# Ordering the FFN weights' preparation on VectorE behind the first inner k blocks

## The chip, the cores and the metric

The kernel runs on one core of a Trainium2 chip. The metric is the device time of one execution in microseconds (us). A core has five engines that run their own instruction queues side by side: TensorE (PE; PEld is its weight load), VectorE (DVE), ScalarE (ACT), GpSimd (POOL) and SyncE (SP, here a queue that only issues transfers). Semaphores order instructions of different engines; instructions of one engine follow each other.

## The reference

A graph layer of 384 nodes with 1024 features, followed by a gated FFN whose weights and activations are quantised to 8 bits. Cut to what matters here:

```
q = x @ wq.T + bq;  k = ...;  v = ...            # x after a layer norm
q2 = (q @ wiq.T + biq) in 16 heads of 64;  k2 = (k @ wik.T + bik);  v2 = (v @ wiv.T + biv)
scores = q2 @ k2.T / 8 + mask                     # mask: -inf where there is no edge
x = x + (softmax(scores) @ v2) @ wo.T + bo

def weight_fake_quant(w):                         # one scale per row
    scale = max(abs(w), axis=1) / 127
    return clip(round(w / scale), -128, 127) * scale

h = act_fake_quant(silu(xq @ wfq(w_gate).T) * (xq @ wfq(w_up).T))    # xq: quantised layer norm of x
out = x + h @ wfq(w_down).T                       # w_gate, w_up: 352 x 1024; w_down: 1024 x 352
```

## The kernel before

The first phase makes q, k, v and q2. Two output blocks of 128 features at a time are computed by a scheme with seven products instead of eight (`project2`): sums of weight halves (`left_sums`, L169 to L173) and of activation quarters (`right_sums`, L157) go in, and VectorE and ScalarE combine the seven results (L200 to L224). Each product is four matmuls of a 128x192 result, shown as eight records[...]. The function takes turns with other VectorE work: the sums for the next pair and the building of the edge mask (L412 to L422), which GpSimd scatters to memory (L425) and reads back (L439).

The second phase is attention in eight head pairs p (L667 on). For p the kernel computes scores (L603), adds the mask and takes the row minimum on VectorE (L609), takes the exponential on ScalarE (L613), normalises on VectorE (L621, L623), turns the result on TensorE (L633), copies it on ScalarE (L635) and multiplies with v2 (L641). Between these steps TensorE is filled with other matmuls: in even p a quarter of v2 (`inner_v`, L580, evacuated by VectorE at L586), in odd p the next two k2 blocks (`inner_k`, which calls `project2`). The first two k2 blocks, `inner_k(0)`, are made ahead of the loop: L664 and L665. The weights of the next `inner_k` are loaded at L79, those of `inner_v` at L570.

The preparation of the FFN weights is a generator, `ffn_weights`. There are fourteen row units: three of w_gate, three of w_up, eight of w_down. For each one, `load_row` (L517) issues the load of a row block into one of three buffers named `row`, two units ahead; `quantise_rows` takes the row maximum on VectorE (L496, tile `wmx`), scales it (L497), takes the reciprocal (L499, tile `wrs`), multiplies on ScalarE with an 8-bit result (L502, tile `w8b`, one buffer) and turns it to bf16 on VectorE (L504, tile `wqi`). When the generator is next advanced, TensorE transposes it (L533 or L540) and ScalarE copies the result out (L534, L541, L542). A `row` buffer is free for the next load when its L502 has run.

`prepare` (L701) advances that generator at fixed points of the loop over p: three times in p = 0, once in p = 1 and 3, twice in the others.

What sets the order: TensorE, SP and GpSimd keep the order in which the program text issues instructions in the whole kernel (a manual schedule for these three). VectorE and ScalarE are ordered by the text in the first phase only up to the loop's set-up; from the end of that context a planner orders their instructions at build time by its own costs. It may move an instruction of the preparation ahead of instructions that the text has earlier, when its operands allow it. In the built program the first L496 stands in the last but one pair of q2's projection, far ahead of the place where `prepare` is called, and four L496 more lie ahead of the last sum of `inner_k(0)`. The loads of the third and later row blocks stand in SP's queue where the text has them; the loads of the second `inner_k`'s weights stand behind the fourth and fifth row loads, which wait for the first and second L502.

Of the kernel before, what the change touches and what calls it, by code (L numbers as in the profile page):

```python
# [28 lines left out]
ALU = mybir.AluOpType  # L29
# [27 lines left out]
def row_bcast(ap, n):  # L57
    return bass.AP(tensor=ap.tensor, offset=ap.offset, ap=[[0, P], [1, n]])
# [3 lines left out]
def gnn_ffn_kernel(ctx: ExitStack, tc: tile.TileContext, a: dict, out: bass.AP):  # L62
    nc = tc.nc
# [13 lines left out]
    def load_w(name, j):  # L77
        wt = w.tile([P, F], F32, name="wt")
        nc.sync.dma_start(wt, a[name][j])  # L79
        return wt  # L80
# [97 lines left out]
    def project2(wa, wb, sums, right, da, db, bias_a, bias_b, pool, name, aside=None):  # L178


        half = HK * P
        s1, s2 = sums
        b11, b21, b22, t1, t2, t3, t4 = right
        a1, a2, b1, b2 = da[:, :HN], da[:, HN:], db[:, :HN], db[:, HN:]

        def product(left, r):
            z = pool.tile([P, HN], F32, name=name)
            for k in range(HK):
                nc.tensor.matmul(  # L189
                    z, left[:, k * P : (k + 1) * P], r[:, k, :], start=(k == 0), stop=(k == HK - 1)  # L190
                )
                yield
            return z

        def other():
            if aside:
                aside()

        def add(dst, z, b, with_):
            nc.vector.scalar_tensor_tensor(dst, z, b, with_, op0=ALU.add, op1=ALU.add)  # L200

        z = yield from product(wa[:, :half], b11)
        nc.scalar.copy(a1, z)  # L203
        other()
        z = yield from product(s2, t2)
        nc.vector.tensor_add(b1, z, a1)
        other()
        z = yield from product(wa[:, half:], b21)
        add(a1, z, bias_a, a1)
        nc.vector.tensor_sub(wa[:, half:], wa[:, half:], s2)  # L210
        other()
        z = yield from product(s1, t1)
        nc.scalar.activation(b2, z, AF.Identity, bias=bias_b)  # L213
        add(a2, z, bias_a, b1)
        other()
        z = yield from product(wb[:, :half], t3)
        nc.vector.tensor_add(b1, z, b1)
        nc.vector.tensor_add(b2, b2, b1)
        other()
        z = yield from product(wa[:, half:], b22)  # L220
        nc.vector.tensor_add(a2, z, a2)
        other()
        z = yield from product(wb[:, half:], t4)
        add(b1, z, bias_b, b1)  # L224
        other()
        yield

    def in_turn(*steps):
        steps = list(steps)
        while steps:  # L230
            for s in list(steps):
                try:
                    yield next(s)
                except StopIteration:
                    steps.remove(s)

    def run(steps):
        for _ in steps:
            pass
# [6 lines left out]
    with ph1_stack:  # L246
# [208 lines left out]
        for i, (name, o) in enumerate(todo[:-1]):  # L455
            (wa, wb), sums = wq_next, sums_next
            right, dst, cols = work[name]
# [49 lines left out]
    def ffn_weights():  # L507

        units = [(name, m, ic) for m, name in enumerate(("L0_ffn_w_gate", "L0_ffn_w_up")) for ic in range(3)]
        units += [("L0_ffn_w_down", 2, c) for c in range(KC)]  # L510
        ahead = []

        def load_row():
            name, m, j = units[len(ahead)]
            i0, rows = ICS[j] if m < 2 else (j * P, P)
            wn = rows_p.tile([P, F], F32, name="row")
            nc.sync.dma_start(wn[:rows, : F if m < 2 else I], a[name][i0 : i0 + rows, :])  # L517
            ahead.append(wn)

        load_row()  # L520
        load_row()
        for u, (name, m, j) in enumerate(units):
            wn = ahead[u]
            if len(ahead) < len(units):
                load_row()
            if m < 2:
                i0, rows = ICS[j]
                wT = (wgT, wuT)[m]
                wq = quantise_rows(wn, rows, F, w_scale[:rows, m, j : j + 1])
                yield  # L530
                pt = ps_tp.tile([P, KC, P], BF16, name="tp")
                for k in range(KC):
                    nc.tensor.transpose(pt[:, k, :rows], wq[:rows, k * P : (k + 1) * P], ident_b[:rows, :rows])  # L533
                nc.scalar.copy(wT[:, :, i0 : i0 + rows], pt[:, :, :rows])  # L534
            else:
                wq = quantise_rows(wn, P, I, wd_scale[:, j : j + 1])
                yield
                pt = ps_tp.tile([P, 3, P], BF16, name="tp")
                for ic, (i0, rows) in enumerate(ICS):
                    nc.tensor.transpose(pt[:rows, ic, :], wq[:, i0 : i0 + rows], ident_b)  # L540
                nc.scalar.copy(wdT[:, 0:2, j * P : (j + 1) * P], pt[:, 0:2, :])  # L541
                nc.scalar.copy(wdT[:96, 2, j * P : (j + 1) * P], pt[:96, 2, :])  # L542

    with ExitStack() as ph:
# [4 lines left out]
        def inner_k(p):  # L549

            k2 = pair_p.tile([P, 2, N], F32, name="k2")
            if p == 0:
                (wa, wb), sums = wq_next, sums_next
            else:
                wa, wb = (load_w("wik", p + j) for j in range(2))
                sums, steps = left_sums(wa, wb, turned)
                run(steps)
            b0 = 4 * KC + p
            return k2, project2(
                wa, wb, sums, k_right, k2[:, 0], k2[:, 1], bias[:, b0 : b0 + 1], bias[:, b0 + 1 : b0 + 2],  # L560
                ps_mm, "mm",
            )
# [85 lines left out]
        def out_group(wo, t, g, ks, pm):  # L648
            gs = slice(g * 512, (g + 1) * 512)
            for k in ks:  # L650
                nc.tensor.matmul(  # L651
                    pm, outT[:, k, t * P : (t + 1) * P], wo[k][:, gs], start=(k == 0), stop=(k == KC - 1)
                )
                yield

        def take(steps, n):
            for _ in range(n):
                if next(steps, "end") == "end":
                    return

        NP = H // 2
        prep = ffn_weights()

        k2_next, first = inner_k(0)  # L664
        run(first)  # L665
        e_before = None
        for p in range(NP):  # L667
            if p % 2 == 0:
                k2 = k2_next
            sc = scores(q2[:, p], k2[:, p % 2])  # L670
            wg = weigh(p - 1, e_before) if p else iter(())
            if p == NP - 1:
                early = [(t, g, ps_mm.tile([P, 512], F32, name="mm")) for t, g in ((0, 0), (0, 1))]
                fill, n = (s for t, g, pm in early for s in out_group(wo, t, g, range(NP - 2), pm)), 2 * (NP - 2)
            elif p % 2:
                k2_next, fill = inner_k(p + 1)
                n = 7 * HK + 1
            else:
                fill, n = inner_v(p // 2), NT * KC
            if p == NP - 2:  # L680

                x = act.tile([P, NT, F], F32, name="actT")
                bo_b = w.tile([P, F], F32, name="wt")
                nc.sync.dma_start(bo_b, row_bcast(a["L0_gnn_bo"], F))
                for t in range(NT):
                    nc.sync.dma_start(x[:, t, :], a["x"][t * P : (t + 1) * P, :])
                for t in range(NT):
                    for g in range(2):
                        gs = slice(g * 512, (g + 1) * 512)
                        nc.vector.tensor_add(x[:, t, gs], x[:, t, gs], bo_b[:, gs])  # L690
                wo = [load_w("wo", k) for k in range(KC)]
            done = 0

            def fill_to(sixteenths):
                nonlocal done
                upto = n * sixteenths // 16
                take(fill, upto - done)
                done = upto


            def prepare(at):  # L701
                if at in ((2, 6, 12) if p == 0 else (2,) if p in (1, 3) else (2, 14)):
                    take(prep, 1)


            fill_to(3 if p % 2 else 2)
            prepare(2)
            next(sc)
            for m in (6, 9, 12):
                fill_to(m)  # L710
                prepare(m)
                take(wg, 1)
            fill_to(14)
            prepare(14)
            run(fill)

            e_before = next(sc)
            take(wg, 1)
# [285 lines left out]
```

## Time and profile before

| what | value |
|---|---|
| time, median of 3 runs | 375.97 us (375.29 to 376.20) |
| the profiled execution | 376.68 us, its span 374.9 us |
| mean granted TensorE clock | 0.994 |
| PE busy | 358.8 us, 96% of the span |
| VectorE busy | 260.2 us, 69% |
| ScalarE busy | 112.8 us, 30% |
| TensorE waited for VectorE's L171 | 1.8 us, once |
| VectorE's L496 | 14 times, 11.4 us busy, 9.5 us idle before |

Busy time is the time in which an engine runs an instruction; the span goes from the first instruction to the last. The chain of waits is followed back from the last instruction and tells which engine sets the end at each time. A busy share of 96% on TensorE means that time can be lost or won only where TensorE stands still, some 16 us in all, 10 of them in the last 31 us.

### The profile page before, as it was taken

The page shows a single profiled execution, that of the slowest core. Times are in us where ns is not written, and L with a number is a line of the kernel's source. Part 1 is how long each engine was busy: PE and PEld are TensorE (multiplying, and loading weights), DVE is VectorE, ACT ScalarE, POOL GpSimd, SP SyncE. Part 2 cuts the span into 40 slices and gives each one's busy share as a digit, 9 for nine tenths or more (in the row PEclk, how much of TensorE's full clock was granted, in tenths as well). Part 3 has the DMA queues.
Part 4 walks back from the last instruction along what each step waited for, and adds up shares of the span by engine and source line. Part 5 has one row for each costly group of instructions (what it writes and reads, how often), then busy time and mean ns, then how long its engine had stood idle before and what let it go on. Part 6 is the DMA issues. An engine that isn't in the chain of part 4 may idle for free.

```text
span 374.9 us, 5872 instructions
## 1 busy us (share of the span) xinstructions
PE 358.8 (96%) x2113; PEld 298.9 (80%) x2113; DVE 260.2 (69%) x788; ACT 112.8 (30%) x264; POOL 72.1 (19%) x81
## 2 busy tenths in 40 slices
PE   8999999999999999799999999999999999999981
PEld 7899999999999999698877878686866545449660
DVE  5868888878889985998487457717492521199785
ACT  2152000100000000123672546446444523034330
POOL 6110254455444544210000000000000000000003
PEclk9999999999999999999999999999999999999997
DMA  8995433343333357148070040040294000000004
GB/s 236 393 376 213 150 114 112 116 133 114 112 112 115 112 170 247 57 119 289 21 231 32 19 129 23 18 171 1 101 375 132 31 0 2 0 0 3 1 0 168
DMA packets 17805, 44.50 MB, mean 119 GB/s; under 512 B 3263, under 2 KB 8401, under 8 KB 17393
## 3 DMA queue, kind: packets, MB, share of 16 engines
q1 hardware_dynamic: 15104, 39.46, 31.1%
q0 software_dynamic: 2672, 4.68, 4.2%
q8 instruction: 16, 0.26, 0.3%
q14 instruction: 13, 0.10, 0.1%
HBM read 41.91 MB, written 2.21 MB: 118 GB/s over the span
## 4 chain that ended last, share of the span: by engine, by line
PE 76%; DVE 12%; DMA 6%; ACT 3%; issue 1%; SPq 0%; DVEq 0%; ACTq 0%
PE p L189 34%; PE mm L580 7%; PE mm L189 6%; PE sc L641 4%; PE tp L633 4%; PE mm L651 3%; PE sc L651 3%; PE mm L814 3%; PE sc L603 3%; PE mm L303 3%; DMA row<-in_L_ffn_w_gate_dram 2%; DMA row<-in_L_ffn_w_down_dram 2%; DMA wt<-in_wik_dram 2%; PE sc L814 1%; DVE s L609 1%; DVE wmx L496 1%
## 5 line engine op out<-in xcount | busy, mean ns | idle before, releaser
L425 POOL DMA_INDIRECT mask_d<-value,place x51 | 56.9, 1115 | 66.3 <-DVE place L422 50.8
L189 PE MATMUL p<-actT,wt 128*128 128x192 f32 x360 | 65.9, 326 | 0.5 <-DVE actT L200 0.5
L189 PEld LDWEIGHTS p<-actT,wt 128*128 128x128 f32 x360 | 59.6, 190 | 0.8 <-DVE actT L200 0.8
L580 PE MATMUL mm<-wt,actT 128*128 128x256 f32 x192 | 46.1, 384 | 0.0
L580 PEld LDWEIGHTS mm<-wt,actT 128*128 128x128 f32 x192 | 34.8, 190 | 7.8 <-issue 2.2
L613 ACT ACTIVATE e<-s,mn 128x384 f32<-128x384 f32 x48 | 29.0, 605 | 26.4 <-DVE mn L609 26.4
L609 DVE CUSTOM_DVE_ANT_0 s<-sc,mask 128x384 f32<-128x384 f32 x48 | 24.5, 551 | 13.0 <-PE sc L603 12.8
L189 PE MATMUL p<-x_right,s 128*128 128x192 f32 x176 | 32.2, 326 | 0.0
L189 PE MATMUL p<-x_right,wt 128*128 128x192 f32 x176 | 32.2, 326 | 0.0
L831 POOL MEMSET hT<- 128x384 f32 x1 | 0.4, 418 | 156.9 <-PE sc L641 156.9
L189 PEld LDWEIGHTS p<-x_right,s 128*128 128x128 f32 x176 | 29.2, 190 | 0.0
L189 PEld LDWEIGHTS p<-x_right,wt 128*128 128x128 f32 x176 | 29.2, 190 | 0.0
L635 ACT COPY eTs<-tp 128x384 f32<-128x384 f32 x48 | 20.5, 478 | 25.3 <-PE tp L633 25.3
L412 DVE SCALAR_TENSOR_TENSOR junk<-key_b,key,later 128x384 f32<-128x384 f32 (+3 forms) x51 | 27.5, 539 | 0.0
L203 ACT COPY actT<-p 128x192 f32<-128x192 f32 x15 | 4.8, 319 | 66.9 <-PE p L189 66.9
L200 DVE SCALAR_TENSOR_TENSOR actT<-p,bias,actT 128x192 f32<-128x192 f32 x45 | 18.7, 415 | 8.5 <-PE p L189 6.6
L213 ACT ACTIVATE actT<-p,bias 128x192 f32<-128x192 f32 x15 | 6.3, 422 | 52.7 <-PE p L189 52.7
L633 PEld LDWEIGHTS tp<-ident,e 128*128 128x128 f32 x144 | 17.1, 140 | 4.9 <-issue 2.4
L633 PE MATMUL tp<-ident,e 128*128 128x128 f32 x144 | 19.7, 273 | 0.3 <-ACT eTs L635 0.3
L603 PE MATMUL sc<-k,actT 64*128 64x384 f32 x96 | 19.9, 518 | 0.0
L189 PE MATMUL mm<-actT,wt 128*128 128x192 f32 x96 | 18.9, 329 | 0.0
L496 DVE TENSOR_REDUCE wmx<-row 128x1 f32<-128x352 f32 (+2 forms) x14 | 11.4, 815 | 9.5 <-DMA row<-in_L_ffn_w_down_dram 6.4
(215 smaller groups left out, 596.3 us busy)
## 6 DMA issues: line engine op xcount, KB each, us to landing
wt<-in_wq_dram SPq DMA_DIRECT2D x8, 512.0 KB, 11.1
wt<-in_wk_dram SPq DMA_DIRECT2D x8, 512.0 KB, 4.3
wt<-in_wv_dram SPq DMA_DIRECT2D x8, 512.0 KB, 4.3
wt<-in_wiq_dram SPq DMA_DIRECT2D x8, 512.0 KB, 4.0
wt<-in_wik_dram SPq DMA_DIRECT2D x8, 512.0 KB, 4.5
wt<-in_wiv_dram SPq DMA_DIRECT2D x8, 512.0 KB, 5.3
wt<-in_wo_dram SPq DMA_DIRECT2D x8, 512.0 KB, 7.5
actT<-in_x_dram SPq DMA_DIRECT2D x6, 512.0 KB, 4.4
```

What stands on the lines that cost most here:

```text
L189: nc.tensor.matmul(z, left[:, k * P : (k + 1) * P], r[:, k, :], start=(k == 0), stop=(k == HK - 1))
L200: nc.vector.scalar_tensor_tensor(dst, z, b, with_, op0=ALU.add, op1=ALU.add)
L412: nc.vector.scalar_tensor_tensor(junk[:, :left], keys[:, (c - k0) * P : (c - k0) * P + left], key[:, c : c + 1], later[:, :left], op0=ALU. ...
L425: ins = nc.gpsimd.indirect_dma_start(out=mask_d, out_offset=bass.IndirectOffsetOnAxis(ap=place[:, c : c + 1], axis=0), in_=value[:, c : c ...
L496: nc.vector.tensor_reduce(mx[:rows], wn[:rows, :n], axis=AX.X, op=ALU.max, apply_absolute_value=True)
L580: nc.tensor.matmul(pm, vT[:, k, t * P : (t + 1) * P], wt[k // HK][:, k0 : k0 + 256], start=(k == 0), stop=(k == KC - 1),)
L603: nc.tensor.matmul(ps[t, h], q2[hs, t * P : (t + 1) * P], k2[hs, :], start=True, stop=True)
L609: nc.vector.tensor_tensor_reduce(s, ps[t, h], mask[:, t, :], -SCALE, 3.0e38, op0=ALU.add, op1=ALU.min, accum_out=mn[h][:, t : t + 1],)
L613: nc.scalar.activation(e[h][:, t, :], s, AF.Exp, bias=mn[h][:, t : t + 1], scale=-1.0, accum_out=sm[h][:, t : t + 1],)
L633: nc.tensor.transpose(pt[:, t * P : (t + 1) * P], e[h][:, t, m * P : (m + 1) * P], ident)
L635: nc.scalar.copy(eT[h][m], pt)
L651: nc.tensor.matmul(pm, outT[:, k, t * P : (t + 1) * P], wo[k][:, gs], start=(k == 0), stop=(k == KC - 1))
```

## The change

The sum that ends a pair of blocks (L224) is kept in a list, and after `inner_k(0)` has been issued its last entry is taken. Every advance of the preparation is then issued under a context that gives each instruction of the same engine (VectorE) that it traces an edge to this sum. The edge holds for the planner's order only: both instructions are VectorE's, so it needs no semaphore. Instructions of the other engines that the advance issues get no edge. Lines below the change move by three.

```diff
         def add(dst, z, b, with_):
-            nc.vector.scalar_tensor_tensor(dst, z, b, with_, op0=ALU.add, op1=ALU.add)
+            return nc.vector.scalar_tensor_tensor(dst, z, b, with_, op0=ALU.add, op1=ALU.add)
...
         z = yield from product(wb[:, half:], t4)
-        add(b1, z, bias_b, b1)
+        last_add.append(add(b1, z, bias_b, b1))
         other()
         yield
+
+
+    last_add = []
...
         k2_next, first = inner_k(0)
         run(first)
+        k2_done = last_add[-1].ins
...
             def prepare(at):
                 if at in ((2, 6, 12) if p == 0 else (2,) if p in (1, 3) else (2, 14)):
-                    take(prep, 1)
+
+                    with tc.issue_after(k2_done):
+                        take(prep, 1)
```

In the built program the orders of TensorE, SP and GpSimd are unchanged. On VectorE the first L496 now directly follows the last sum of `inner_k(0)`, two of them in a row, and then come the first scores' steps; the whole preparation up to the second k2 blocks is later by the same measure. The sums of the second pair's weights (L169 to L173), which stood before the first scores' steps, now stand after all of the first pair's scores. On ScalarE the first L502 moves from the first phase to behind the first exponential. From the last sum of the second pair of k2 blocks on, VectorE's order is the same as before.

## Prediction

> **What bounds the kernel now.** I read the page's busy shares first (PE busy for 96% of the span), then the chain of work that ended last in order of time. Its columns are start us, length us, and engine, tile and line:
>
> ```profile
> 23.94 118.32 PE p L189 x728
> 142.28 0.38 SPq L570
> 142.71 7.54 DMA row<-in_L_ffn_w_gate_dram
> 150.28 1.22 DVE wmx L496
> 151.50 0.33 DVE actT L200
> ...
> 152.61 1.13 DVE wmx L496
> ...
> 154.55 0.61 DVE s L171
> 155.20 8.07 PE p L189 x48
> ```
>
> TensorE carries the end alone for 118 us; then the path goes through a transfer of an FFN weight row and two row maxima on VectorE. So VectorE's queue stands still for data that nothing needs yet, and TensorE's sums stand behind it. The timelines of TensorE, VectorE and SP's queue give the sizes (start us, duration, ..., in brackets the idle time before):
>
> ```profile
> 149.88 1.46 PE L189 MATMUL p<-right,wt 128*128 128x192 f32 x8
> 151.88 1.57 PE L189 MATMUL p<-actT,wt 128*128 128x192 f32 x8 [0.53 <-DVE actT L200]
> 155.20 1.57 PE L189 MATMUL p<-right,s 128*128 128x192 f32 x8 [1.75 <-DVE s L171]
> ...
> 172.88 1.46 PE L580 MATMUL mm<-wt,actT 128*128 128x256 f32 x6
> ...
> 178.45 0.61 PE L533 MATMUL tp<-ident_b,wqi 128*128 128x128 bf16 x8
> ...
> 188.27 0.49 PE L189 MATMUL mm<-k_right,s 128*128 128x192 f32 x2
> ...
> 194.44 1.57 PE L189 MATMUL mm<-actT,s 128*128 128x192 f32 x8 [0.71 <-DVE k L206]
> ```
>
> ```profile
> 150.28 1.22 DVE L496 TENSOR_REDUCE wmx<-row 128x1 f32<-128x1024 f32 x1 [2.67 <-DMA row<-in_L_ffn_w_gate_dram]
> ...
> 173.52 0.69 DVE L169 TENSOR_TENSOR s<-wt 128x512 f32<-128x512 f32 x1 [1.37 <-DMA wt<-in_wik_dram]
> ```
>
> ```profile
> 156.90 9.77 SPq L517 DMA_DIRECT2D row<-in_L_ffn_w_up_dram  x2
> 166.77 1.19 SPq L79 DMA_DIRECT2D wt<-in_wik_dram  x2
> ```
>
> In the regular stretch a product (eight records of L189) starts every 1.30 us. From 149.88 to the first L580 at 172.88 are 15 products: 19.50 us at that pace, so 169.38. The loss is 172.88 - 169.38 = 3.50 us, of which the two bracketed waits and their restarts make 2.72 and late evacuations in the first k blocks the rest (starts at 167.00, 168.60, 170.00, 171.47, 172.88 instead of every 1.30).
>
> **What the Trainium skill says.** "TensorE: Matmul & The Clock Gate", section on the array's architectural detail: VectorE's and ScalarE's queues are strict FIFOs. The trace agrees: at 151.41 L200 runs only once L496 is through, though its operands were there. The same page, "What's actually happening": the array's clock falls after an idle window of about 3.4 us. TensorE's 1.75 us wait left the granted clock at 1.00 in that window, and none of the waits below exceeds 2 us, so I charge no clock. "DMA: Bandwidth & Descriptors", "Queues, rings and completion order": one issuing engine's descriptors are consumed in ring order on each DMA engine. The trace fits: x's first 512 KB landed 3.38 us after its issue with more loads right behind it, while x's third part, behind two weights, took 9.2.
>
> **What the change removes: -3.50 us.** In the built order, every VectorE step of the FFN preparation (L496, L497, L499, L504) now follows the last L200 of inner_k(0). Before, five L496 and their followers stood ahead of or among those sums. Removed from the queue between 147.6 and 174 are the 2.67 us wait for the row, five L496 of 1.13 us from start to start, two L504 of 0.60 and a dozen small ones. Walking the remaining VectorE work from 147.6 with the starts of the same rows (L157 0.47, L169/L171/L173/L210 0.60, L200 0.33, L217/L218 0.27), every sum is ready before its product: s of the last wiq pair at 151.0 against 152.5 needed, the last k_right piece at 161.3 against 168.1. TensorE therefore keeps 1.30 us and reaches L580 at 169.38. No semaphore is added for the edge; SP, POOL and PE keep their order.
>
> **What it adds, step 1: the transposes of the first weights wait.** TensorE does three L580 matmuls (1.38), four scores (1.49), six L580 (2.70) and stands at 174.95 before L533. VectorE: last L200 at 169.61; then by start-to-start times L496 x2 2.26, L497 0.06, one softmax step L609 0.48, L499 0.07, three L609 1.43, L497 0.06, L496 1.14, L499 0.07, L586 0.34, L504 0.60 (0.68 busy). Sum: 169.94 + 6.59 = 176.53; TensorE goes on at 176.6. It was 178.45, so 1.85 is left and 1.65 is paid here. ScalarE's L502 of these weights comes after the first exp: 173.55 to 174.7, hidden.
>
> **Step 2: the transfers that hang on L502.** The row loads at L517 wait for L502 of the row whose buffer they take, and SP's queue holds the load of the next wik pair (L79) behind two of them. Copy L534 starts 0.65 after L533 (177.25), takes 0.92; the second L502 1.15: 179.32. Then row, wik, wik are issued. Before, they were issued from 166.33 and the second wik landed at 173.5, 7.17 us later; so now at 186.5. Before there was slack: TensorE used it at 188.27. Now it is late. L169 186.5, +0.61, L621 and L499 0.16, L171 at 187.27; 0.74 after L171's start TensorE had its product at 155.20, so 188.0. TensorE arrives at 186.4 (176.6 + 0.45 + 3.94 + 0.45 + 2.74 + 0.85 + 1.30 = 186.33) and waits 1.7. It was 188.27: only 0.26 is left.
>
> **Step 3: VectorE from there to the second k blocks.** It has no idle time left: L171 0.60, three L623 0.99, L621 0.09, L173 0.60, three L623 0.99, four L609 1.91, L206 0.27, L504 0.60, L496 1.13, L200 0.33, L210 0.60, L497 0.06, L496 0.45, L499 0.07, L169 0.61 = 9.31, so the L200 that frees the bank of the sixth product starts at 196.58 and frees it at about 197.05. TensorE by itself would be there at 188.0 + 8.55 = 196.55. Before, the sixth product began at 197.80. The 0.71 us wait at 194.44 disappears (L206 at 192.45, TensorE at 193.3), which is why 0.26 grows to 0.75. Then the sequence of VectorE's instructions is the same as before, the down rows follow ScalarE as before (last gating row issued at 197, landing 2.3 later, used at 200), and TensorE-bound work passes the gain on. Sum: -3.50 + 1.65 + 1.6 - 0.5 = **-0.75 us**. The profiled execution took 376.68 us (span 374.9), so 375.9 for its like; on the median of 375.97: **375.2 us**.
>
> **Unknown sizes.** The landing of wik is the term that matters: each us moves the result by one. If it landed at 185.8, VectorE itself is ready no sooner (scores done at 184.9, two L609, L497): the result is -1.4, 374.6; step 1's gain of 1.85 is a floor, 374.1. On the other side, landing at 187.2 leaves nothing.
>
> **Rivals.**
> - More survives: row and wik land sooner because nothing else moves then, or VectorE's queue is shorter than summed. The bandwidth speaks for it: 342 to 363 GB/s in the 2 us slices from 168 to 172, against up to 440 elsewhere. 374.1 to 374.8. Chance 0.30.
> - The whole 3.50 survives, 372.5: the order says no, since both waits of steps 1 and 2 are real operands. Chance 0.05.
> - Slower: wik shares its way with what SP now issues right behind it. Before, the third up row and two wiv parts came 4.5 and 4.9 us after the row; now at 180.7 and 181.2, while wik is moving. If all five go together, 0.52 + 1.05 + 0.39 + 1.05 = 3.0 MB at 350 GB/s are 8.6 us, with 0.7 to the first bytes and 1.4 from last byte to use: landing at 190.0, 3.5 later, 378.7. It decides from a landing after 188.4 (over 9 us after the row's issue). Against it: x's first part, above. Chance 0.17, with milder forms.
> - Nothing: VectorE's chain of step 3 is some tenths longer, 375.8 to 376.9. Chance 0.08. That the edge doesn't act is excluded by the order.
>
> **Numbers.** My case (0.40) spans 374.6 to 375.8. 0.3% (about what a measurement of this kernel can tell from no change) is 1.13 us: below 374.84 lie 0.13 of my case and the two faster ones, 0.48; within it 0.27 + 0.08 = 0.35; slower 0.17. The range 374.0 to 376.9 leaves out the 0.05 and most of the 0.17.
>
> **What would show it.** Right: no wait of L496 before the first L580, which starts near 169.4; TensorE idle 1.6 us before L533 near 175 (releaser L504), idle about 1.7 before L189 near 187 (releaser L171 behind the wik transfer), sixth product near 197. Wrong: the second wait absent, or wik landing well over 8 us after the row's issue, or later stretches that change in length.

## The result, and the profile after

The changed kernel takes 377.07 us (median of 15 executions, 376.30 to 379.17) against 375.97 us of the kernel before (15 executions beside it, 375.20 to 377.33). The ratio is 1.0035, its 95% interval 1.0021 to 1.0048: slower by about a third of a per cent, where 375.2 us and a gain had been predicted. Two further comparisons, told below, gave 1.003 (1.0015 to 1.0045) and 1.0057 (1.0035 to 1.008). The profiled execution after took 378.0 us, its span is 376.2 us, its mean granted clock 0.989 (before: 376.68, 374.9 and 0.994).

The timeline of TensorE after (start us, duration, line and tiles, in brackets the idle time before and what ended it), with lines three further than before:

```profile
149.84 1.46 PE L189 MATMUL p<-right,wt 128*128 128x192 f32 x8
...
169.34 1.46 PE L583 MATMUL mm<-wt,actT 128*128 128x256 f32 x6
...
176.48 0.62 PE L536 MATMUL tp<-ident_b,wqi 128*128 128x128 bf16 x8 [1.40 <-DVE w_scale L500]
...
188.62 0.59 PE L189 MATMUL mm<-k_right,s 128*128 128x192 f32 x2 [2.15 <-DVE s L171]
...
189.49 2.33 PE L606 MATMUL sc<-k,actT 64*128 64x384 f32 x8
191.75 2.11 PE L189 MATMUL mm<-k_right,s 128*128 128x192 f32 x6
193.70 0.81 PE L189 MATMUL mm<-actT,wt 128*128 128x192 f32 x4
...
198.91 0.49 PE L189 MATMUL mm<-actT,wt 128*128 128x192 f32 x2
```

Fifteen products now take 19.50 us, with no wait: what the edge was to remove is removed. The first transposes wait and start at 176.48. (The bracket names L500, VectorE's next instruction, 176.34 to 176.48, which TensorE does not need; what the transposes read is `wqi`, which L507 just before it wrote, 175.74 to 176.42.) Up to there the kernel is ahead. The second product of the second k blocks then starts at 188.62, where the kernel before had it at 188.27, after a wait of 2.15 us. Behind it, scores and products take 4.21 us (189.49 to 193.70) which take 2.57 us in another execution of the same kernel (run e9 below, whose lines are one further):

```profile
189.49 1.56 PE L607 MATMUL sc<-k,actT 64*128 64x384 f32 x8
...
192.06 0.81 PE L190 MATMUL mm<-actT,wt 128*128 128x192 f32 x4
```

The chain of waits of the first profile says what ended the 2.15 us:

```profile
178.04 1.16 ACT w8b L505
...
179.22 0.33 SPq L520
...
179.65 0.37 SPq L79
...
180.52 6.61 DMA wt<-in_wik_dram
...
187.98 0.60 DVE s L171
...
188.62 0.59 PE mm L189 x2
```

The second weights' load (wik) stands behind the row load, which waits for ScalarE's step of the row in its buffer; wik is used 7.93 us after the row's issue at 179.22. And the slow microseconds behind the wait show in the table of short windows (columns: window, length, TensorE's busy time, granted clock, DMA share, GB/s):

```profile
189.00:190.00 1.00, 1.00 (x14) 1.00 1.09 345
190.00:191.00 1.00, 1.00 (x8) 0.57 1.06 327
191.00:192.00 1.00, 1.00 (x5) 0.50 1.07 350
192.00:193.00 1.00, 1.00 (x4) 0.50 0.91 352
193.00:194.00 1.00, 1.00 (x6) 0.73 0.93 356
194.00:195.00 1.00, 1.00 (x10) 1.00 0.32 127
```

Read as time at 1.00 and time at 0.50, the column gives 0.86 + 1 + 1 + 0.54 = 3.4 us of halved clock, from about 190.1 on, 1.5 us after TensorE had restarted. It makes the scores and products 1.64 us longer. At the next scores (L606 near 202) 1.25 us of that are left: they start 13.65 us after the second product, in e9 12.40.

Executions begin the undisturbed stretch at slightly different times, so I count from here on from the start of one product, the reference product, which stands near 138.2 to 138.8 in every profile (138.18 in the first of before, 138.14 in the first of after). Sums over executions and kernels are then comparable.

### The profile page after: what moved, and what is told of

Read it like the earlier page. It is cut to its first block, busy times and chain, and to the rows that moved or that the text cites. A ratio compares the mean times of both kernels' runs of the same rounds, so it can differ in the third digit from the quotient of the medians.

```text
span 376.2 us, 5867 instructions
## 1 busy us (share of the span) xinstructions
PE 359.6 (96%) x2112; PEld 300.3 (80%) x2113; DVE 261.6 (70%) x788; ACT 112.7 (30%) x264; POOL 73.9 (20%) x81
## 4 chain that ended last, share of the span: by engine, by line
PE 81%; DVE 10%; DMA 4%; ACT 2%; issue 2%; SPq 0%; DVEq 0%; ACTq 0%
PE p L189 36%; PE mm L189 9%; PE mm L583 7%; PE tp L636 4%; PE sc L606 4%; PE sc L644 3%; PE mm L654 3%; PE sc L654 3%; PE mm L820 3%; PE mm L306 3%; DMA wt<-in_wik_dram 2%; DMA row<-in_L_ffn_w_down_dram 2%; PE sc L820 1%; DVE y L953 1%; DVE actT L694 1%
## 5 line engine op out<-in xcount | busy, mean ns | idle before, releaser
L428 POOL DMA_INDIRECT mask_d<-value,place x51 | 58.6, 1148 | 62.3 <-DVE place L425 42.5
L583 PE MATMUL mm<-wt,actT 128*128 128x256 f32 x192 | 46.1, 384 | 0.0
L583 PEld LDWEIGHTS mm<-wt,actT 128*128 128x128 f32 x192 | 34.8, 190 | 7.8 <-issue 2.2
L606 PE MATMUL sc<-k,actT 64*128 64x384 f32 x96 | 20.6, 536 | 0.0
L626 DVE TENSOR_SCALAR e<-e,rs 128x384 f32<-128x384 f32 x48 | 17.2, 414 | 0.4
```

Source lines behind the costliest of these rows:

```text
L428: ins = nc.gpsimd.indirect_dma_start(out=mask_d, out_offset=bass.IndirectOffsetOnAxis(ap=place[:, c : c + 1], axis=0), in_=value[:, c : c ...
L583: nc.tensor.matmul(pm, vT[:, k, t * P : (t + 1) * P], wt[k // HK][:, k0 : k0 + 256], start=(k == 0), stop=(k == KC - 1),)
L606: nc.tensor.matmul(ps[t, h], q2[hs, t * P : (t + 1) * P], k2[hs, :], start=True, stop=True)
L626: nc.vector.tensor_scalar(e[h][:, t, :], e[h][:, t, :], rs[:, t : t + 1], None, op0=ALU.mult)
```

## The experiments

Three questions were open: whether the profile of before from which the prediction was made is typical; what the wait for wik costs; what the clock costs.

**The kernel before again (e1, and later e11 and e12).** No edit.

> The kernel before, unchanged, profiled and timed once more. Theory A (the profiled execution of before was typical): from the start of the product at 149.9 to the first L580 again 23.0 us, 3.5 more than fifteen products at 1.30 us, with L496 waiting about 2.7 us for its row; the time is 376.0 +- 0.5 and its executions' mean clocks are those of the profile, 0.994 to 0.997. Theory B (before was profiled in a slow moment, so that the change removed less than the 3.50 us of my sum): the stretch is shorter by 0.5 us or more, with a shorter wait of L496.

Measured: 376.1 us, ratio 0.9996 (0.9983 to 1.001). TensorE's timeline in its profile:

```profile
154.60 1.57 PE L189 MATMUL p<-right,s 128*128 128x192 f32 x8 [1.75 <-DVE s L171]
...
172.41 1.46 PE L580 MATMUL mm<-wt,actT 128*128 128x256 f32 x6
...
187.81 0.49 PE L189 MATMUL mm<-k_right,s 128*128 128x192 f32 x2
```

As theory B has it, the same program loses less here: one of the two waits before the first L580 is gone, since L496 waited 1.90 us for its row and not 2.67. The first L580 comes 34.05 us after the reference product instead of 34.70, and the second product 49.45 instead of 50.09. Two further profiles were taken later to see which is common.

> The kernel before once more, for its profile alone. Counted from the start of the undisturbed product near 138.2, the first L580 came after 34.70 us in the profile that the prediction was made from and after 34.05 in the second one, the second product of the second k blocks after 50.09 and 49.45. If the first was a late execution, 33.9 to 34.3 and 49.3 to 49.7 are expected here; if the two are equally common, either.

> As the run before it: 33.9 to 34.3 and 49.3 to 49.7 if the first profile of before was a late execution.

They gave 33.95 and 33.60 for the first L580, 49.35 and 49.00 for the second product (the last is earlier still than expected). So the profile of the prediction was the latest of four: 34.70 against a mean of 34.08. What moves it is the row's landing: L496 starts 12.10, 11.32, 11.27 and 10.92 us after the reference, in the order of the L580. In five profiles of the changed kernel's order (its own three, and two kernels below that leave work out later on) the first L583 comes after 31.19 or 31.20 us: that dependence on a transfer is gone.

Two more profiles bear on the base: the two kernels with further loads, told below (e13 and e14), are the kernel before up to the first L580. It comes after 34.28 and 32.82 us there, the second product after 49.67 and 48.22. With them the means are 33.90 and 49.30, so the base of the sums below is uncertain by about 0.2 us.

**TensorE kept busy during the wait (e2).** Seven transposes of the identity, whose result nothing reads, between the first and the second product of the second k blocks; they take 0.93 us:

```diff
+            if p == 1:
+                take(fill, HK)
+                done = HK
+                pt = ps_tp.tile([P, P], F32, name="tp")
+                for _ in range(7):
+                    nc.tensor.transpose(pt, ident, ident)
             fill_to(3 if p % 2 else 2)
```

> The changed kernel with seven transposes of the identity (about 0.77 us of TensorE work) put between the first and the second product of the second k blocks, where TensorE waits 2.15 us for s2. Nothing else moves: VectorE's and ScalarE's orders are the same. Theory C (the granted clock, which the profile after shows at 0.5 from 190.4 to 193.5 us, falls because TensorE was idle that long): with the idle time cut to about 1.4 us no execution shows the mean clock of 0.989 and the kernel gets faster by 0.3 to 1.2 us on the changed one (377.1), to 376 to 376.8, although work was added. Theory T (what costs is the wait for the wik transfer alone): no change, 376.8 to 377.4, and executions at 0.989 as before.

Measured: 377.08 us, ratio 1.0029 (1.0016 to 1.0042). The wait left is 0.88 us, and only 4 of 22 executions have a mean clock of 0.992 or less, where 7 of the 15 of the changed kernel had. This count is rough: the profiled execution is one of the four, and its trace shows a clock of 1.00 in the whole stretch from 170 to 200 us; its low mean (0.992) comes from the last 10 us. Yet the median is the same, so neither theory came true in whole. The halved clock isn't the whole loss: the second product still starts 49.97 us after the reference, and the 18 executions with a higher mean clock have a median of 377.05 us.

**The wik loads issued early (e3),** behind the first three rows, so that no wait of ScalarE's stands ahead of them:

```diff
-                wa, wb = (load_w("wik", p + j) for j in range(2))
+                wa, wb = k_early.pop() if k_early else (load_w("wik", p + j) for j in range(2))
...
             prepare(2)
+            if p == 0:
+                k_early.append([load_w("wik", 2 + j) for j in range(2)])
             next(sc)
```

> The changed kernel with the loads of the second k blocks' weights (wik) issued right behind the first three FFN rows in SP's queue, ahead of the rows that wait for L505 (L502 before). Theories C and T both: the wait of 2.15 us before the second product vanishes; with the 1.40 us wait before the first transposes left, TensorE reaches the second product near 186.4 instead of 188.6 and the kernel takes 374.2 to 375.2. If the transfer was not what TensorE waited for in the end (VectorE's queue alone, theory Q), the second product stays later than 187.9 and the time above 376.

Measured: 375.71 us, ratio 0.9979 (0.9968 to 0.999), above the expected band but faster than the kernel before. No execution of 22 has a mean clock of 0.992 or less. The wait for L171 is gone, the 1.40 us wait for the transposes stays:

```profile
186.85 0.49 PE L189 MATMUL mm<-k_right,s 128*128 128x192 f32 x2
```

This is 48.24 us after the reference product. Against e2 on the same chip the kernel takes 1.37 us less, and its ratio of 0.9979 stands against 1.003 to 1.0057 of the changed kernel: the late load of wik, with the clock that follows the wait, is what turns the gain into a loss. The miss of half a microsecond does not lie at the second product, which comes where it was expected (186.4 in the count of the first profile is 48.26). It lies behind it: to the next scores 13.09 us pass, where it is 12.40 in the changed kernel with an undisturbed clock, and TensorE waits there for VectorE twice (0.33 us for L206, 0.32 us for L217). At these scores the kernel is 0.81 us ahead of the mean of before.

This run does not move the load alone: the planner now places the sums of these weights (L169 to L173) at 166.11 to 167.91, ahead of the first scores' steps. How much of the wait is the transfer's shows in VectorE's line in the first profile of the changed kernel:

```profile
187.15 0.69 DVE L169 TENSOR_TENSOR s<-wt 128x512 f32<-128x512 f32 x1 [1.04 <-DMA wt<-in_wik_dram]
```

VectorE stands 1.04 us for wik; until then it is busy with the scores. In all six profiles of the changed kernel's order (its own three, e2, e8, e10) it comes to L169 after 47.96 to 48.00 us and stands there 0.29 to 1.24 us, 0.8 in the mean. With wik there in time and the order unchanged, the second product would come 1.47 us later, at about 49.4, no earlier than in the kernel before (49.47). So, as an estimate from these numbers, the late transfer costs 0.8 us of step 2, and the rest of that wait is the late place of the sums in VectorE's queue.

**The edge set earlier (e4),** to the last sum of the last pair of q2 instead of the first k blocks':

```diff
-        k2_next, first = inner_k(0)
-        run(first)
-        k2_done = last_add[-1].ins
+        k2_done = last_add[-1].ins
+        k2_next, first = inner_k(0)
+        run(first)
```

> The changed kernel with the edge tied to the last sum of q2's last pair instead of the last sum of inner_k(0): the preparation comes some 9 us earlier, into VectorE's idle time among the first k blocks (5 us idle there in the profile after), but not in front of q2's sums. If the place of the edge decides (all theories): the products before the first L583 keep 1.30 us, no wait before the first transposes, the wik loads are issued near 167 and nothing waits for them: 372.8 to 374.2 with theory A, 373.8 to 375.2 with theory B. If the row maxima between the k sums hold up the banks as before, 0.3 to 0.7 us of it are lost.

Measured: 373.85 us, ratio 0.9937 (0.9916 to 0.9959), 6 executions: faster than both kernels. Its profile, TensorE's timeline:

```profile
169.92 1.46 PE L583 MATMUL mm<-wt,actT 128*128 128x256 f32 x6
...
175.49 0.61 PE L536 MATMUL tp<-ident_b,wqi 128*128 128x128 bf16 x8
...
185.31 0.49 PE L189 MATMUL mm<-k_right,s 128*128 128x192 f32 x2
```

Neither of the two new waits is there, and the k blocks lose only 0.32 us (first L583 after 31.52 instead of 31.20). The reason is in VectorE's timeline of the changed kernel (the repeated one, below): within the first k blocks VectorE stands idle for 1.77 + 0.89 + 0.73 + 0.43 + 0.55 + 0.94 = 5.31 us, the two largest of them here:

```profile
163.57 0.36 DVE L206 TENSOR_TENSOR k<-mm,k 128x192 f32<-128x192 f32 x1 [1.77 <-ACT k L203]
164.82 0.42 DVE L200 SCALAR_TENSOR_TENSOR k<-mm,bias,k 128x192 f32<-128x192 f32 x1 [0.89 <-PE mm L189]
```

The edge of the change keeps the row maxima out of this idle time and puts them where TensorE waits for VectorE. The earlier edge lets the first of them (161.50) into it; the row in front of wik is issued at 168.64 instead of 179.22.

**Both of these (e7):** the edits of the last two diffs together.

> The edge anchored at the last sum of the last q2 pair, and the second weights (wik) loaded ahead of the gated rows. With the earlier anchor alone, wik was issued at 169.1 and its product did not wait, so if wik's landing mattered only through that wait, the earlier load adds nothing: 373.5 to 374.2, ratio 0.993 to 0.9955. If earlier sums of these weights also ease VectorE's later queue (the 0.72 us wait behind L206 near 191.5), up to 0.7 less: 372.9 to 373.5.

Measured: 373.81 us, ratio 0.9941 (0.9921 to 0.9961), as expected for "adds nothing": the wait behind L206 near 191.7 is still 0.87 us.

**The changed kernel again (e5),** unaltered.

> The changed kernel once more, unaltered, beside the kernel before on the same chip. Theory W (the second weights' load takes back what step 1 leaves): ratio 1.001 to 1.004, TensorE reaches the first L583 within 0.2 us of 19.5 us after the product that starts near 150, the second product of the second k blocks starts at 188.0 to 188.7 with about 2 us of idle time ended by L171, against 187.8 to 188.3 in the two profiles of before; so the advance of 1.5 to 2.0 us that stands at L536 (176.5 against 178.0 to 178.5) is gone at that product. Theory C (the granted clock falls after that wait and sets the loss): again about half of the executions have a mean clock of 0.992 or less, and those at 0.995 or more are no longer than the spans of before; ratio then 1.000 to 1.004.

Measured: 376.72 us against 376.02, ratio 1.003 (1.0015 to 1.0045). First L583 after 31.20 us, first L536 after 38.34, both as in the first profile; the second product at 188.35 with a wait of 1.40 us, after 49.74. Five of 22 executions have a mean clock of 0.992 or less (median 378.27 us, the others 376.52). In the first comparison it was 7 of 15, with 378.0 against 376.8. Of 166 executions of the kernel before whose clock was recorded with these runs, 3 are that low, and their times (374.26, 375.19 and 375.54) are not long. Theory W is right in its numbers but for the wait, shorter than said; of theory C the low clock is right, in fewer executions than half, but the other executions are slower than before as well.

**The rows loaded earlier, without an edge (e6):** the kernel before, with the first three row loads ahead of the wiv loads (the generator is started ahead of the first phase for this, which the lines below do not show).

```diff
-        load_row()
-        load_row()
+        for _ in range(3):
+            load_row()
+        yield
...
-            if len(ahead) < len(units):
+            if 3 <= u + 3 - 1 < len(units) and len(ahead) < u + 3:
                 load_row()
```

> The kernel before with no edge; the first three FFN weight rows are loaded ahead of the wiv loads, so that no row maximum waits for its transfer (the planner then places the maxima some 15 instructions earlier on VectorE). Theory D (what before loses is the wait of VectorE's queue for the row, 1.9 to 2.7 us of it): TensorE's wait near 154.6 to 155.2 shrinks below 0.7, the first L580 is at 170 to 171.5, and since nothing is moved behind the sums nothing is paid later: 374.0 to 375.3. Theory E (the work of the five maxima itself, 1.13 us each, ahead of and among the sums is what counts): the sums are still late, the first L580 at 172 or later: 375.7 to 376.6.

Measured: 376.16 us, ratio 1.0014 (1.0001 to 1.0027), in theory E's band. But the timelines show that this is no clean test. VectorE's, and then TensorE's:

```profile
142.97 1.22 DVE L496 TENSOR_REDUCE wmx<-row 128x1 f32<-128x1024 f32 x1 [2.43 <-DMA row<-in_L_ffn_w_gate_dram]
```

```profile
150.25 1.57 PE L189 MATMUL p<-actT,wt 128*128 128x192 f32 x8 [0.89 <-DVE wt L210]
...
154.90 1.57 PE L189 MATMUL p<-right,s 128*128 128x192 f32 x8 [0.48 <-DVE s L171]
...
172.46 1.46 PE L584 MATMUL mm<-wt,actT 128*128 128x256 f32 x6
```

The planner moved the maximum up along with the load, and it waits 2.43 us for the row there. How the loss of before divides between that wait and the work of the maxima stays open; the removed total, 34.08 - 31.20, does not depend on it.

**Without the loads behind wik (e8), and with more of them (e13, e14).** The second slice of v2 uses the wik tiles, so the two wiv loads (1.0 MB) are not issued:

```diff
+                kept_k.append([wa, wb])
...
             for j in range(2):
+                if c == 1:
+                    wt = kept_k[-1]
+                    break
                 wt.append(w.tile([P, F], F32, name="wt"))
```

> The changed kernel without the two loads of the second wiv slice, 1.0 MB issued right behind wik; the products of that slice use the wik tiles instead, so a quarter of the values is not the reference's. Instructions on VectorE and ScalarE keep their order. Theory S (wik shares its way with what is issued behind it): wik is used 7.1 to 7.5 us after the row's issue instead of 7.9, and the second product's wait is 0.4 to 0.8 shorter; the whole 0.4 to 1.0 us less than the changed kernel, 376.0 to 376.7. Theory L (7.9 us is what the row and wik take by themselves after a pause): still 7.8 to 8.0, wait about 2.1, 376.8 to 377.3.

Measured: 377.21 us, ratio 1.0034 (1.0017 to 1.0051), a low clock in 7 of 17 executions; wik is used 7.60 us after the row's issue, the wait is 1.81 us. This lies between the bands of the two theories and within what the changed kernel's order shows elsewhere, so theory S has nothing from it. A row load was still behind, so the reverse was tried: the kernel before with two loads of 512 KB that nothing reads, right behind wik.

```diff
+    spare = [ffn_w.tile([P, F], F32, name=f"spare{j}") for j in range(2)]
...
                 wa, wb = (load_w("wik", p + j) for j in range(2))
+                if p == 2:
+                    for s in spare:
+                        nc.sync.dma_start(s, a["wik"][2])
```

> The kernel before, with two further loads of 512 KB each (a copy of a weight that nothing reads) issued by SP right behind the second inner k weights (wik). In four profiles of before, with nothing behind them for 3 us, L169 used wik 7.06 to 7.18 us after the issue of the fifth row; in six of the changed kernel or of kernels with its order, with a row and two wiv parts 0.4 to 1.5 us behind, after 7.19 to 8.17 us. Theory S (loads issued behind slow the ones ahead): 7.5 to 8.3 us here. Theory L (the longer time of the changed kernel comes from something else, such as the pause of the queue before it): 7.0 to 7.3 us. TensorE does not wait for wik in this kernel, so the time itself should stay within 375 to 377.5.

> The same kernel for a second profile: 7.5 to 8.3 us by theory S, 7.0 to 7.3 by theory L.

Measured: 6.92 and 6.79 us (first profile: the row at 157.00 + 9.76 - 0.33 = 166.43, and the line of VectorE below), 376.91 and 374.78 us.

```profile
173.35 0.69 DVE L169 TENSOR_TENSOR s<-wt 128x512 f32<-128x512 f32 x1 [1.21 <-DMA wt<-in_wik_dram]
```

These two loads, issued 2.0 us after the row, did not delay wik. Why wik takes 7.2 to 8.2 us in the changed kernel's order and 7.06 to 7.18 in four profiles of the kernel before isn't explained. One thing goes with it: in all six of these profiles the load of a row block of 96 rows is issued 1.9 to 2.1 us after the row ahead of wik, and in the kernel before about 4.5 us after it. The kernel with the earlier edge (e4) fits: that load comes 1.9 us after the row there, and wik is used after 8.06 us (168.64 to 176.70). No run takes this load away, so its part is not shown.

**A longer wait with less work (e9, e10).** The first product of the second k blocks is cut short; TensorE then arrives earlier at the same wait, and nothing else moves.

```diff
-        def product(left, r):
+        def product(left, r, m=HK):
...
             for k in range(HK):
-                nc.tensor.matmul(
+                if k < m:
+                    nc.tensor.matmul(
...
-        z = yield from product(wa[:, :half], b11)
+        z = yield from product(wa[:, :half], b11, first)
...
-                ps_mm, "mm",
+                ps_mm, "mm", first=2 if p == 2 else HK,
```

> The changed kernel, but the first product of the second k blocks has four matmuls instead of eight (the other half of its sum is left out), so TensorE arrives 0.65 us earlier at the product that waits for wik's sums, and the wait there is 2.0 to 2.8 us instead of 1.4 to 2.15; nothing else is moved. Theory C (a wait of about 2 us or more there lets the granted clock fall): the share of executions with a mean clock of 0.992 or less rises from 19 of 54 to more than 6 in 10, and the median is 377.4 to 378.6 although less is computed. Theory N (the low clock comes from elsewhere): share about a third as before, median 376.5 to 377.2.

> The same with two matmuls of eight: the wait is 2.4 to 3.1 us. Theory C: low clock in 8 of 10 executions or more, median 377.8 to 378.8. Theory N: about a third, 376.5 to 377.2.

Both texts count the product wrongly: `HK` is 4, and the eight records are four matmuls. So e9, with 4 for the 2 in the diff, left nothing out and is the changed kernel a third time; e10 left out two matmuls of four, which makes TensorE 0.65 us early and not 0.97.

Measured: e9 378.04 us, ratio 1.0057 (1.0035 to 1.008), low clock in 5 of 8 executions. The changed kernel has then a mean clock of 0.992 or less in 7 of 15, 5 of 22 and 5 of 8, together 17 of 45. e10, with less work: 378.36 us, ratio 1.006 (1.0043 to 1.0078), low clock in 18 of 20. TensorE's timeline of e10, whose lines are one further, and its table of short windows (window, length, busy time of PE, PEld, DVE, ACT and POOL, granted clock, DMA share, GB/s):

```profile
189.11 0.59 PE L190 MATMUL mm<-k_right,s 128*128 128x192 f32 x2 [3.03 <-DVE s L171]
```

```profile
189.00:190.00 1.00, 0.89 (x12) 0.75 (x12) 1.00 (x5) 0.70 (x1) 0.00 (x0) 0.99 1.10 351
190.00:191.00 1.00, 1.00 (x6) 0.70 (x6) 1.00 (x5) 0.80 (x1) 0.00 (x0) 0.50 0.71 189
```

The longer TensorE waits here, the more often the mean clock is low: at most 4 of 22 executions where the profile has a wait of 0.88 us, 17 of 45 at 1.40 to 2.15, 18 of 20 at 3.03. That is theory C for the clock. Only profiled executions show their wait, so which waits the 17 had is not known. In the profile of e9 a wait of 2.14 us left the clock at 1.00 throughout, in the first one a wait of 2.15 halved it; nothing in the traces tells the two apart. The kernel before waits for L171 in its first phase, 0.86 to 1.76 us in six profiles (those of e13 and e14 counted), and only 3 of 166 executions are low. So waits of that length were hardly ever, if at all, followed by a low clock at that place. Whether their length alone decides was not tested.

## Why the prediction was wrong, step by step

Counted from the reference product, means of four profiles of before stand against the profiles of the changed kernel's order:

| step, as the prediction had it | predicted, us | measured, us | from |
|---|---|---|---|
| removed up to the first L580/L583 | -3.50 | -2.88 | 34.08 to 31.20 |
| step 1, transposes wait | +1.65 | +1.57 | first L533 39.65, first L536 38.34: 1.31 of 2.88 left |
| step 2, loads behind ScalarE's step | +1.6 | +2.09 | second product 49.47 to 50.25: 0.78 behind |
| step 3, VectorE to the second k blocks' end | -0.5 | -0.27 | second product to L603/L606: 12.67 to 12.40 |
| clock | 0 | +0.5 | 17 of 45 executions, with medians 1.05 to 1.75 us above the others |
| sum | -0.75 | +1.0 | |

50.25 is the mean start of L171 in six profiles (the three of the kernel, e2, e8, e10) plus the 0.73 us from there to the product; 12.40 is from the profiles with an undisturbed clock (e5, e8, e9). The sum of 1.0 stands beside 1.1 us between the medians of the first comparison, 0.7 of the second and 2.1 of the third, which has only eight executions of the changed kernel. Behind these scores nothing differs: from there to the end of the span it is 174.10 us in the mean of before and 174.09 in that of the changed kernel's three profiles.

**What was right.** The mechanism of every step: no wait before the first L583 (predicted at 169.38, measured 169.34), a wait before the transposes (176.6 and 176.48; 1.6 expected idle, 1.40 measured), a wait for L171 behind the wik transfer with its row issued at 179.22 (predicted 179.32), VectorE without idle time behind it (sixth product 9.05 us after the second by the working, 8.94 measured in e5). The Trainium skill's statement on strict FIFOs ("TensorE: Matmul & The Clock Gate", the array's architectural detail) agrees with e4, which issues the same instructions, in another order on VectorE and ScalarE alone, and takes 2.5 us less than the kernel before.

**"Removed: -3.50 us"** is the first step that failed. It is right for the profiled execution and 0.62 too large for the mean one. Step 3 has the same fault: the profile of the prediction took 12.88 us from the second product to the next scores, where the mean is 12.67, and 12.88 - 12.40 is the 0.5 predicted. That execution took 376.68 us, 0.71 more than the median, and the whole of the sum was still subtracted from the median. The time alone would not have told: the third profile of before belongs to an execution of 376.92 us and has its first L580 at 33.95.

**"The second wik at 186.5"** is the second. The 7.17 us from row issue to use were measured in one profile of before, where the four lie within 7.06 to 7.18; in the new place it took 7.93, 7.92, 7.42, 7.19 and 8.17 in the five profiles with the same loads, 7.60 in e8: 0.54 more in the mean. The prediction said itself that each us there counts in full and that at 187.2 nothing would be left (187.15 in the first profile); its sum carried a duration from one place to another as if it were fixed. Why it is longer stays open. "DMA: Bandwidth & Descriptors", section on queues, rings and completion order, which the prediction used for its x example, is not contradicted: two 512 KB loads right behind wik did not delay it (6.92 and 6.79).

**"I charge no clock"** is the third. The Trainium skill, "TensorE: Matmul & The Clock Gate", section "What's actually happening", speaks of an idle window of about 3.4 us and of windows that run freely. The low stretch fits that length: 3.4 us in the first profile. But there an idle time of 2.15 us was enough, and 17 of 45 executions of this kernel, whose three profiles show idle times of 1.40 to 2.15 us, have the low mean clock; the measurement decides. The 1.75 us in the first phase of the kernel before had shown nothing, and from it the prediction took that its own wait of 1.7 us was free. At the new place it was up to 2.15.

**The rivals.** The sign was that of the slower rival, but not its mechanism: it needed wik later than 9 us after the row, the most that was seen is 8.17, and loads behind it were not shown to slow it. (It reckoned 0.7 us to the first bytes and 1.4 from the last byte to use. The trace of before has about 0.9 and 1.6: row issued at 166.34, first bytes after 167.25, the 1.57 MB through at about 171.9, use at 173.52.) The rival "more survives" needed wik by 185.8; with wik early (e3), that is, without this wait at all, 375.71 was measured beside 376.40 of before. That is 0.7 less, where this rival called for 1.2 to 1.9: at the second product e3 is 1.23 ahead of before, and 0.42 of it are lost behind it. The rival "nothing" wanted a longer chain of step 3; it was not longer.

## What to carry to other kernels

An order edge that takes work out of one queue's way also delays whatever hangs on that work: list the buffers that this work frees and the transfers queued behind them, and put the edge where the engine has idle time for the work. Here VectorE stood idle for 5.3 us in the stretch that the edge protected, and the same edge one step earlier gained 2.5 us instead of losing 1.1. A sum made on one profile carries that execution's lateness; where a step depends on when a transfer lands, take two or three profiles of before, if they are to be had.

## What the runs showed that was not expected

TensorE's clock was halved after a standstill of 2.15 us, shorter than the stretch of low clock that followed: 3.4 us, beginning 1.5 us after the restart in the first profile and 0.9 us in that of e10. In the first profile it cost 1.64 us at once and 1.25 us by the next scores. A low mean clock was seen in at most 4 of 22 executions with a wait of 0.88 us in the profile, in 17 of 45 with 1.40 to 2.15, in 18 of 20 with 3.03, and in none of 34 of the three kernels without that wait (e3, e4, e7).
